# A fused graph layer on one core: results leave in block order, and the second half of the n gate is copied out of PSUM by ScalarE at once

## The chip, the cores and the metric

The kernel runs on one core of a Trainium2 chip. The metric is the device time of one execution in microseconds; for the kernel before it is the median of three runs. The engines are named as in the profile: PE is TensorE (PEld its weight loads), DVE is VectorE, ACT is ScalarE, POOL is GpSimd, and SP is SyncE, which here only issues DMAs.

## The reference, cut to what matters

For 64 graphs of 256 nodes with 256 channels each, one layer of a gated graph network is computed in float32:

```python
h   = maximum(layernorm(x), 0)                                  # x: (64, 256, 256)
c   = relu(bn1(conv1d_1tap(h)))
xc  = relu(bn2(conv1d_17taps(c)) + h)                           # along the 256 nodes
s   = h @ w_se.T + b_se                                         # 3 features per node
A   = exp(-|s_n - s_m|^2) * adj
xn  = A @ relu(h @ w_msg.T + b_msg)
gi  = concat(xc, xn) @ w_ih.T + b_ih                            # three gates of 256
gh  = h @ w_hh.T + b_hh
r   = sigmoid(gi_r + gh_r); z = sigmoid(gi_z + gh_z)
n   = tanh(gi_n + r * gh_n)
out = x + (1 - z) * n + z * h
```

## The kernel before, in words

**Tiling.** Graphs are worked on in pairs (a pair is called i, 32 of them), and four pairs make a block of eight graphs (b, 8 of them). A tile of a pair has channels on the 128 partitions, in two halves (dc 0 and 1), and 512 columns: the 256 nodes of one graph and then of the other. The nodes are not in their natural order there. The 17-tap convolution is done by a transform over 16 places in each half block of nodes, so that columns run in the order (q, h, b), while the rows of x and of the output in DRAM run in the order (b, h, c).

**The block.** The loop at line 1321 does the convolution of a block first: `begin(m)` and `complete(m)` (lines 941 and 948) multiply transformed inputs (tiles `Sv`, `V`, `U`, `PT`) with transformed filters. The filters were put in DRAM (`filt`) at the start by `filter_steps` and are loaded again for each block, one 128x512 tile after the other, into nine slots `wb` by `load_kinds` (line 905) on SP's queue. Then, pair by pair, come `sums`, the r and z gates and the n gate (`gates`, line 1181). Each gate pair is a matrix product in a seven-product form (`seven`, line 1155) in two PSUM tiles of two banks each, `acc0` and `acc1`: `opened(0, A)` and `opened(1, E)` evict them. During the gates the nine slots `wb` hold sums, tanh values (`tz`) and a temporary (`e`). At the end of a block `give` (lines 1475 and 1476) frees them, and `load_kinds()` starts the loads for the next block's first products, which go into `acc0` and `acc1` again.

**The n gate.** The function `n` (line 1190) evicts one PSUM tile in two steps: ACT writes half 1 plus its bias to `gn`; DVE multiplies that with r; then DVE's second instruction reads half 0 of the same PSUM tile and adds it. Only after this last read may PE open a new sum in the tile. After tanh and three DVE instructions the result stands in `tr`, and ACT copies it as two planes of 16 bits each to `back` (lines 1202 to 1204).

**Delivery.** `finish` (line 1245) turns `back` on SP's queue by a DMA transpose into `gn`; `deliver` (line 1260) has ACT merge the 16-bit planes back into rows of float32 in `back`, and then POOL's queue adds x to them in flight (a load with `accum_op`, line 1268) and stores them (line 1269), per graph one load and one store of 256 KB. Both address DRAM through `rows` (line 588), a pattern of 8 by 16 pieces of 2 KB; `blocks` (line 609) has the same pieces in sequence. For the last pair of a block the delivery comes in the middle of the next block.

**What sets the order.** No instruction is issued where it is written. The `Recorder` (line 250) notes all of them, gives each a cost and, for DMAs, a size (lines 341 to 369), computes from the order of TensorE's work when each is due, plays a list schedule with these costs (`plan`, line 388), and emits in that order. An engine then works strictly in the order it was given. So a changed cost or a changed pattern can move instructions everywhere. `filter_steps` (line 1278) is called with (1, 2, 3, 3) steps after the first four pairs at the start.

Of the kernel before, what the change touches and what calls it, by code (L numbers as in the profile page):

```python
# [14 lines left out]
U16 = mybir.dt.uint16  # L15
AF = mybir.ActivationFunctionType
ALU = mybir.AluOpType
# [232 lines left out]
class Recorder:  # L250
# [83 lines left out]
    def record(self, engine, op, args, kw):  # L334
        method = getattr(getattr(self.nc, engine), op)
        out = kw["out"] if "out" in kw else args[0]
        ins = [v for v in list(args) + list(kw.values()) if isinstance(v, bass.AP) and v is not out]
        n = 1
        for s in out.shape[1:]:
            n *= s  # L340
        size = 0
        if op.startswith("dma"):
            if "transpose" in op:
                size, cost = 2.5, self.TURN
            elif "accum_op" in kw:
                size, cost = 2.3, 1.0
            else:
                k = max(self.share(out, ins[0]), 10 if engine == "gpsimd" else 1)
                run = min(self.run(v) for v in (out, ins[0]))
                size = n * out.shape[0] * WIDTH[out.dtype] * 16 / k / 330e3 * max(1, 1400 / run)  # L350
                cost = 0.35 if k > 10 and run > 1024 else 0.62
        elif engine == "tensor":
            cost = n / 597 + 0.006
            if op == "transpose":
                cost = out.shape[-1] / 1170
            elif args[1].shape[0] < 32:
                cost = 0.23
        elif engine == "vector":
            cost = {"bn_stats": 0.33, "bn_aggr": 0.07}.get(op, n / 960 + 0.07)
            if op == "tensor_mul" and n == 256:  # L360
                cost = 0.5
        elif engine == "scalar":
            cost = n / 1400 + (0.2 if op == "activation" else 0.12)
            if out.dtype == U16:
                cost = n / 860
            elif len(out.shape) == 3 and op == "activation" and n == 256:
                cost = 0.49
        else:
            cost = 1.1 if self.planned == 0 else 7.0 if ALU.pow in args else 2.0
        k = len(self.tasks)  # L370
        self.tasks.append(Task(engine, lambda: method(*args, **kw), cost, size, self.first))  # L371
        self.last[engine] = k
        if self.behind is not None:
            self.tasks[k].preds.add(self.behind)
        if self.first is not None:
            self.first += 1
        for v in ins:
            self.access(k, v, False)
        self.access(k, out, True)
        return k  # L380
# [106 lines left out]
def kernel(  # L487
# [18 lines left out]
    nc = Recorder(tc.nc)  # L506
    P = 128
    B, N, D = x.shape
    G = 2
# [4 lines left out]
    DC = D // P  # L514
# [6 lines left out]
    L = 16  # L521
    NW = N // L
# [65 lines left out]
    def rows(t, g):  # L588
        return t[g].rearrange("(b h c) d -> h b (c d)", h=L // 2, c=MC)

    def row_tile(t, g):
        return t[:, g * MC:(g + 1) * MC, :].rearrange("p c d -> p (c d)")
# [5 lines left out]
    def chunk(t, g, c):  # L598
        return t[:, g * N + c * P:g * N + (c + 1) * P]
# [3 lines left out]
    X, ADJ, HT, XNM, STATS = {}, {}, {}, {}, {}  # L603
# [5 lines left out]
    def blocks(t, g):  # L609
        return t[g].rearrange("(b h c) d -> b h (c d)", h=L // 2, c=MC)  # L610
# [114 lines left out]
    p = aux()  # L725
# [449 lines left out]
    def halfs(p, k):  # L1175
        return p[:, :, k * N:(k + 1) * N]

    def pieces(t):
        return t.rearrange("p (g n) -> p g n", n=N)

    def gates(i, between=None):
        tr, gn = tr_tile, gn_tile
        tz = [slots[ROLE[f"tz{dc}"]].rearrange("p c d -> p (c d)") for dc in range(DC)]

        def rz(dc, p):
            for gate, t in ((0, tr[:, dc]), (1, tz[dc])):
                nc.scalar.activation(pieces(t), halfs(p, gate), AF.Tanh,
                                     bias=b_rz[:, gate * DC + dc:gate * DC + dc + 1], scale=0.5 - dc)

        def n(dc, p):  # L1190
            g = gn[:, dc]
            nc.scalar.activation(pieces(g), halfs(p, 1), AF.Identity,
                                 bias=b_hh[:, 2 * DC + dc:2 * DC + dc + 1], scale=1.0 - 2 * dc)
            nc.vector.scalar_tensor_tensor(g, tr[:, dc], 1.0, g, op0=ALU.add, op1=ALU.mult)
            nc.vector.scalar_tensor_tensor(pieces(g), pieces(g), 0.5, halfs(p, 0), op0=ALU.mult,
                                           op1=ALU.subtract if dc else ALU.add)
            nc.scalar.activation(g, g, AF.Tanh, bias=b_ih[:, 2 * DC + dc:2 * DC + dc + 1])
            d = tr[:, dc]
            nc.vector.tensor_sub(d, HT[i][:, dc], g)
            nc.vector.scalar_tensor_tensor(d, tz[dc], 1.0, d, op0=ALU.add, op1=ALU.mult)  # L1200
            nc.vector.scalar_tensor_tensor(d, d, 0.5, g, op0=ALU.mult, op1=ALU.add)
            u = d.bitcast(U16).rearrange("p (n j) -> p j n", j=2)
            for j in range(2):
                nc.scalar.copy(back.bitcast(U16).rearrange("p (c j n) -> p c j n", c=DC, j=2)[:, dc, j], u[:, j])

        def last(dc, g, p):
            a = slice(g * N, (g + 1) * N)
            v, d = gn[:, dc, a], tr[:, dc, a]
            nc.scalar.activation(v, p[:, N:], AF.Identity,
                                 bias=b_hh[:, 2 * DC + dc:2 * DC + dc + 1], scale=1.0 - 2 * dc)  # L1210
            nc.vector.scalar_tensor_tensor(v, d, 1.0, v, op0=ALU.add, op1=ALU.mult)
            nc.vector.scalar_tensor_tensor(v, v, 0.5, p[:, :N], op0=ALU.mult, op1=ALU.subtract if dc else ALU.add)
            nc.scalar.activation(v, v, AF.Tanh, bias=b_ih[:, 2 * DC + dc:2 * DC + dc + 1])
            nc.vector.tensor_sub(d, HT[i][:, dc, a], v)
            nc.vector.scalar_tensor_tensor(d, tz[dc][:, a], 1.0, d, op0=ALU.add, op1=ALU.mult)
            for c in range(MC):
                t = chunk(y_last[:, dc], g, c).rearrange("p (b h) -> p h b", b=NW)
                u, w = (q[:, c * P:(c + 1) * P].rearrange("p (h b) -> p h b", b=NW) for q in (d, v))
                nc.vector.scalar_tensor_tensor(t, u, 0.5, w, op0=ALU.mult, op1=ALU.add)

        seven(i, RZ, rz)
        if between:
            between()
        if i + 1 < NP:
            seven(i, NH, n)
            return
        a0, p5, e1, a1, e0 = aux(), aux(), aux(), acc()[:, 1], acc()[:, 0]
        e = slots[ROLE["e"]].rearrange("p c d -> p (c d)")
        part(a0, 1, i, NH, True)
        nc.scalar.mul(e0, a0, -1.0)  # L1230
        part(p5, 5, i, NH, True)
        nc.scalar.copy(e, p5)
        part(a0, 2, i, NH)
        last(0, 0, a0)
        part(e0, 6, i, NH)
        nc.vector.tensor_add(a1, e0, e)
        part(e0, 7, i, NH)
        nc.vector.scalar_tensor_tensor(e1, e0, -1.0, e, op0=ALU.mult, op1=ALU.subtract)
        last(1, 1, e1)
        part(a1, 3, i, NH)  # L1240
        last(0, 1, a1)
        part(e0, 4, i, NH)
        last(1, 0, e0)
# [16 lines left out]
    def deliver(i):  # L1260
        y = back.rearrange("p (q d) -> p q d", d=D)
        t = gn_tile.rearrange("p c n -> p (c n)").bitcast(U16)
        v = y.bitcast(U16).rearrange("p q (c d j) -> p j c q d", c=DC, j=2)
        u = t.rearrange("p (c j q d) -> p j c q d", j=2, c=DC, d=P)
        for j in range(2):
            nc.scalar.copy(v[:, j], u[:, j])
        for g in range(G):
            nc.gpsimd.dma_start(out=row_tile(y, g), in_=rows(x, G * i + g), accum_op=ALU.add)
            nc.gpsimd.dma_start(out=rows(out, G * i + g), in_=row_tile(y, g))

    FIRST = PARTS[1][1]
    steps = deque((m, g) for g in range(FIRST) for m in range(len(PASSES)))
# [5 lines left out]
    def filter_steps(n, wide=True):  # L1278
        for _ in range(n):
            banks[0] += 1  # L1280
            p = acc()[:, 0] if wide and banks[0] % 3 == 0 else aux()
            filters(p, *steps.popleft(), nc.gpsimd if len(steps) % 2 else nc.sync)
# [9 lines left out]
    for j in range(PB):  # L1292
        if j > 0:
            norm(j)
        transpose_h(j)
        conv1(j, True)
        split(j)
        filter_steps((1, 2, 3, 3)[j])
    *bn2, b_ih, b_hh = columns("bn2")
    s2, h2_shift = fold_bn(bn2, "bn2", 1.0 / L)  # L1300
    b_rz = keep("b_rz", 2 * DC)
# [19 lines left out]
    for b in range(NB):  # L1321
        i = b * PB
# [25 lines left out]
        if b == 0:  # L1348
# [6 lines left out]
            back = late.tile([P, DC * W], FP, name="back")  # L1355
# [168 lines left out]
```

## Time and profile before

| what | value |
|---|---|
| median of three runs | 1705.13 us |
| the three runs | 1708.3, 1705.13, 1702.14 us |
| the profiled execution: its own time | 1703.87 us |
| its span, first to last instruction | 1702.1 us |
| mean granted TensorE clock | 0.994 |
| DVE busy | 1457.8 us (86%) |
| ACT busy | 1052.4 us (62%) |
| POOL busy | 231.8 us (14%) |
| DMA moved | 261.47 MB, mean 154 GB/s |

The profile is of one execution. A row of a group names the tile that is written and the tiles that are read; then come the number of instructions, the microseconds that they were busy together, the mean nanoseconds of one, and the idle time of the engine just before them with what ended it. A row of a timeline has the start, the length, the engine, the instruction, how many were merged, and in brackets the idle time before it. Since one helper records everything, every instruction has the same line, L371; groups are told apart by their tiles.

### The profile page before, as it was taken

The numbers are of one execution on the slowest core, as the hardware profiler recorded it, in microseconds if no ns is written. First come the engines' busy times: TensorE is split into PE (matmuls) and PEld (weight loads), VectorE is DVE, ScalarE is ACT, GpSimd is POOL, SyncE is SP. The second block draws the span as 40 slices with busy tenths as digits, with TensorE's granted clock in tenths as the row PEclk, the third lists the DMA queues.
The fourth block names the chain that finished last, engine by engine and source line by source line (L and its number), as shares of the span: only waits on it lengthen the run. The fifth ranks groups of instructions, "written<-read, shape, count | busy, mean of one in ns | idle before, by whom it ended". The sixth has DMA issues, their size and how long they took to land.

```text
span 1702.1 us, 26181 instructions
## 1 busy us (share of the span) xinstructions
PE 1666.3 (98%) x8984; PEld 1420.8 (83%) x8984; DVE 1457.8 (86%) x3401; ACT 1052.4 (62%) x1967; POOL 231.8 (14%) x245
## 2 busy tenths in 40 slices
PE   8999999999999999999999999999999999999998
PEld 5888878988889788888888887897888978898886
DVE  7969989799889998799997998979987899879545
ACT  5546665685657765676655866567575766556453
POOL 4211130022110121102110021101211012100010
PEclk9999999999999999999999999999999999999999
DMA  9982666966579366773559554694756836484032
GB/s 228 306 280 69 137 117 142 280 136 140 108 196 241 94 127 124 218 208 89 122 113 293 136 116 110 160 273 97 144 112 191 233 91 125 88 245 129 17 60 52
DMA packets 326812, 261.47 MB, mean 154 GB/s; under 512 B 204751, under 2 KB 252139, under 8 KB 326678
## 3 DMA queue, kind: packets, MB, share of 16 engines
q1 hardware_dynamic: 296982, 216.71, 48.4%
q0 software_dynamic: 29280, 42.76, 13.1%
q8 instruction: 71, 1.16, 0.3%
q14 instruction: 63, 0.52, 0.1%
q10 hardware_dynamic: 416, 0.32, 0.1%
HBM read 156.60 MB, written 43.78 MB: 118 GB/s over the span
## 4 chain that ended last, share of the span: by engine, by line
PE 77%; DVE 17%; DMA 3%; issue 1%; ACT 1%; SPq 0%; DVEq 0%; ACTq 0%
PE acc L371 52%; PE aux L371 25%; DVE V L371 3%; DVE T L371 3%; DVE U L371 2%; DVE gn L371 2%; DMA wb<-filt 2%; DVE tr L371 1%; DVE acc L371 1%; DVE wb L371 1%; DVE Yv L371 1%; DVE PT L371 1%; DMA taps<-in_c_wT_dram 1%; DVE msg L371 1%; DMA filt<-Yv 0%
## 5 line engine op out<-in xcount | busy, mean ns | idle before, releaser
L371 PE MATMUL acc<-wb,w_ih 128*128 128x256 f32 x768 | 191.9, 379 | 0.0
L371 PEld LDWEIGHTS acc<-wb,w_ih 128*128 128x128 f32 x768 | 145.9, 190 | 19.8
L371 POOL DMA_DIRECT2D back<-in_x_dram x62 | 61.9, 1161 | 696.6 <-ACT back L371 622.5
L371 POOL TENSOR_TENSOR rstd<-rstd,neg_half 128x4 f32<-128x4 f32 x32 | 81.6, 2548 | 472.7 <-DVE shift L371 284.8
L371 PE MATMUL aux<-wb,w_x 128*128 128x256 f32 x576 | 141.6, 384 | 0.6 <-ACT e L371 0.5
L371 DVE SCALAR_TENSOR_TENSOR V<-T,V 128x128 f32<-128x128 f32 (+2 forms) x448 | 140.2, 377 | 0.0
L371 PE MATMUL acc<-wb,w_x 128*128 128x256 f32 x576 | 136.5, 381 | 1.8 <-DVE acc L371 1.5
L371 PEld LDWEIGHTS acc<-wb,w_x 128*128 128x128 f32 x576 | 107.9, 190 | 28.6 <-DVE acc L371 8.4
L371 PEld LDWEIGHTS aux<-wb,w_x 128*128 128x128 f32 x576 | 108.0, 191 | 20.2 <-issue 4.0
L371 PE MATMUL aux<-w_msg,hT 128*128 128x259 f32 x512 | 120.9, 381 | 0.0
L371 PE MATMUL acc<-V,wb 128*128 128x128 f32 x1024 | 119.0, 275 | 0.6 <-ACT acc L371 0.6
L371 PEld LDWEIGHTS acc<-U,wb 128*128 128x128 f32 x1024 | 117.4, 192 | 1.5 <-issue 0.5
L371 PE MATMUL acc<-U,wb 128*128 128x128 f32 x1024 | 118.2, 275 | 0.3 <-DMA wb<-filt 0.3
L371 PEld LDWEIGHTS acc<-V,wb 128*128 128x128 f32 x1024 | 116.7, 192 | 1.2 <-ACT acc L371 0.8
L371 PE MATMUL acc<-wb,w_hh 128*128 128x256 f32 x384 | 110.1, 381 | 0.7 <-ACT acc L371 0.7
L371 DVE TENSOR_TENSOR T<-Yv 128x512 f32<-128x512 f32 (+1 forms) x80 | 42.5, 580 | 79.4 <-ACT Yv L371 78.9
L371 PE MATMUL aux<-hT,w_c 128*128 128x512 f32 x224 | 107.3, 595 | 2.7 <-ACT e L371 2.7
L371 PE MATMUL acc<-Yv,w_ih 128*128 128x256 f32 x380 | 108.5, 381 | 0.1
L371 PEld LDWEIGHTS aux<-w_msg,hT 128*128 128x128 f32 x512 | 96.5, 190 | 14.3
L371 PE MATMUL acc<-hT,w_hh 128*128 128x256 f32 x380 | 104.7, 383 | 0.6 <-ACT acc L371 0.4
L371 PE MATMUL acc<-xnm,w_ih 128*128 128x256 f32 x380 | 103.9, 380 | 0.0
L371 ACT COPY back<-gn 128x1024 uint16<-128x1024 uint16 x62 | 80.5, 1348 | 36.6 <-DMA gn<-back 36.6
(194 smaller groups left out, 3842.1 us busy)
## 6 DMA issues: line engine op xcount, KB each, us to landing
wb<-filt SPq DMA_DIRECT2D x376, 256.0 KB
back<-in_x_dram POOLq DMA_DIRECT2D x62, 256.0 KB, 7.3
out_dram<-back POOLq DMA_DIRECT2D x62, 256.0 KB, 4.8
x<-in_x_dram SPq DMA_DIRECT2D x58, 256.0 KB
halves_d<-halves SPq DMA_DIRECT2D x28, 512.0 KB
adjh<-halves_d SPq DMA_DIRECT2D x112, 128.0 KB
hh<-halves SPq DMA_DIRECT2D x108, 128.0 KB
filt<-Yv POOLq DMA_DIRECT2D x18, 224.0 KB, 4.6
```

Of the source, the lines that this page charges most:

```text
L371: self.tasks.append(Task(engine, lambda: method(*args, **kw), cost, size, self.first))
```

## The change

Four things change. `deliver` addresses x and the output through `blocks`; for this the two copies of `n` into `back` permute the columns, from the order (q, h, b) that they read to (q, b, h), while they wrote and read them in sequence before. `n` gets a second ACT instruction that copies half 0 of the PSUM tile to the pair's `XNM` tile, whose products are over by then, and DVE's second instruction reads that copy. The planner is told a size of 1.3 in place of 2.3 for an accumulating load. And the calls of `filter_steps` at the start take (0, 2, 3, 4) steps.

```diff
             elif "accum_op" in kw:
-                size, cost = 2.3, 1.0
+                size, cost = 1.3, 1.0
...
             nc.scalar.activation(pieces(g), halfs(p, 1), AF.Identity,
                                  bias=b_hh[:, 2 * DC + dc:2 * DC + dc + 1], scale=1.0 - 2 * dc)
+            x = XNM[i][:, dc]
+            nc.scalar.copy(pieces(x), halfs(p, 0))
             nc.vector.scalar_tensor_tensor(g, tr[:, dc], 1.0, g, op0=ALU.add, op1=ALU.mult)
-            nc.vector.scalar_tensor_tensor(pieces(g), pieces(g), 0.5, halfs(p, 0), op0=ALU.mult,
-                                           op1=ALU.subtract if dc else ALU.add)
+            nc.vector.scalar_tensor_tensor(g, g, 0.5, x, op0=ALU.mult, op1=ALU.subtract if dc else ALU.add)
...
             u = d.bitcast(U16).rearrange("p (n j) -> p j n", j=2)
+            v = back.bitcast(U16).rearrange("p (c j n) -> p c j n", c=DC, j=2)[:, dc]
             for j in range(2):
-                nc.scalar.copy(back.bitcast(U16).rearrange("p (c j n) -> p c j n", c=DC, j=2)[:, dc, j], u[:, j])
+                nc.scalar.copy(v[:, j].rearrange("p (q b h) -> p q b h", h=L // 2, b=NW),
+                               u[:, j].rearrange("p (q h b) -> p q b h", h=L // 2, b=NW))
...
         for g in range(G):
-            nc.gpsimd.dma_start(out=row_tile(y, g), in_=rows(x, G * i + g), accum_op=ALU.add)
-            nc.gpsimd.dma_start(out=rows(out, G * i + g), in_=row_tile(y, g))
+            nc.gpsimd.dma_start(out=row_tile(y, g), in_=blocks(x, G * i + g), accum_op=ALU.add)
+            nc.gpsimd.dma_start(out=blocks(out, G * i + g), in_=row_tile(y, g))
...
         split(j)
-        filter_steps((1, 2, 3, 3)[j])
+        filter_steps((0, 2, 3, 4)[j])
```

## The prediction

> **What bounds the kernel now.** I read the page's busy times first, then PE's groups with their idle time, then timelines where PE stands still.
>
> ```profile
> PE 1666.3 (98%) x8984; PEld 1420.8 (83%) x8984; DVE 1457.8 (86%) x3401; ACT 1052.4 (62%) x1967; POOL 231.8 (14%) x245
> ```
>
> PE is busy for 98% of the span: 1702.1 less 1666.3 leaves 35.8 us of visible idle time, and PE's work is the same in both kernels. So nothing that only speeds DVE, ACT or a DMA can bring more than a part of these 35.8 us. Where they lie, PE's groups by form say:
>
> ```profile
> L371 PE MATMUL acc<-Sv,wb 128*128 128x128 f32 x512 | 67.2, 288 | 14.2 <-DVE tr L371 9.4 <-DMA wb<-filt 2.8 <-DVE gn L371 1.8
> ```
>
> 14.2 us stand before the products that open a block. In PE's timeline the seven block entries (b = 1 to 7) show gaps of 1.75, 2.28, 1.95, 2.40, 2.36, 2.36 and 0.24 us. Three things must be there: the tile acc0 must be free, the first filter must have landed, and PE must be done. The chain of work at the third entry shows which comes last:
>
> ```profile
> 691.05 0.88 PE acc L371 x4
> ...
> 691.94 5.68 DMA wb<-filt
> 697.62 0.14 issue
> 697.76 2.38 PE acc L371 x10
> ```
>
> The filter takes 5.68 us to land. DVE's last read of acc0 is over well before that, so the row's "DVE tr" names an instruction that ended at that moment by chance:
>
> ```profile
> 695.28 0.68 DVE L371 SCALAR_TENSOR_TENSOR gn<-gn,acc 128x512 f32<-128x512 f32 x1
> ```
>
> It ends at 695.96. Why the filter is slow, the queues tell, first for the third entry (POOL, then SP), then for the seventh (POOL, SP, PE):
>
> ```profile
> 684.78 1.96 POOL L371 DMA_DIRECT2D back<-in_x_dram  x2 [27.12 <-ACT back L371]
> 691.27 0.64 POOL L371 DMA_DIRECT2D out_dram<-back  x1 [4.52 <-DMA back<-in_x_dram]
> 693.00 0.63 POOL L371 DMA_DIRECT2D out_dram<-back  x1 [1.09 <-DMA back<-in_x_dram]
> ```
> ```profile
> 691.51 3.92 SPq L371 DMA_DIRECT2D wb<-filt  x7
> ```
> ```profile
> 1493.24 0.64 POOL L371 DMA_DIRECT2D out_dram<-back  x1 [4.54 <-DMA back<-in_x_dram]
> 1494.91 0.63 POOL L371 DMA_DIRECT2D out_dram<-back  x1 [1.03 <-DMA back<-in_x_dram]
> ```
> ```profile
> 1498.02 8.74 SPq L371 DMA_DIRECT2D wb<-filt  x11
> ```
> ```profile
> 1502.56 2.92 PE L371 MATMUL acc<-Sv,wb 128*128 128x128 f32 x24 [0.24 <-issue]
> 1506.05 1.16 PE L371 MATMUL acc<-Sv,wb 128*128 128x128 f32 x8 [0.58 <-DMA wb<-filt]
> ```
>
> At the third entry both stores of the pair before are issued just as the filters are: from the first filter issue (691.51) to the first product (697.76) it takes 6.25 us. At the seventh the stores are 3 to 5 us earlier, and it takes 4.54 us. The 1.7 us between is the gap.
>
> **What the Trainium skill says.** "DMA: Bandwidth & Descriptors", section "Why a DMA increments its semaphore by 16 and not by 1": a DMA runs on the largest number of engines up to 16 that divides the slowest dimension of both sides. The 8x16 pieces of `rows` then give 8 engines, the 128 of `blocks` 16. The trace doesn't name engines; its landing times agree in direction (the block-order load of adj on POOL's queue, also 256 KB, lands in 3.5 us at the median, a store in `rows` order in 4.8, an accumulating load in 7.3). Same page, "Issuing engines are not separate DMA queues": all queues share 16 engines, which fits the two entries above. "Advanced Engine Details and Errata", section "SBUF Cachelines": accesses that go to a new line of 16 bytes each time pay a penalty. The trace shows it on DVE alone (below). "ScalarE: Activation LUTs", section "What ACT_TABLE_LOAD costs": an activation without pointer operands takes 186 ns and 0.833 ns an element, 612 ns for 512; the copies into back take 618.
>
> **The change part by part.**
>
> *Block order, at the entries.* The seventh entry's own rest is 0.24 + 0.58 = 0.82 us. If the other six come to it, they give 13.1 - 6 x 0.82 = 8.2 us. Do the stores get out of the way? A load with accumulation at the third entry takes about 6.2 us from issue (684.78) to the store that waits for it (691.27), 7.6 with its pair (685.4 to 693.00). With twice the engines I put it between the 3.5 us of the adj load and 6.2, at 4.8; so the stores are issued some 1.4 to 2 us earlier, and they take less long themselves. In the new emission order ACT's first merging copy also stands ahead of `wb<-aux`, before which ACT idles 5.69 us. That is 2 to 4 us in all, against the 1.7 us needed. It can't be below nothing: no byte is added.
>
> *PSUM copied at once.* 62 more ACT copies; the row wb<-aux (PSUM, 512 columns) has 584 ns, and successive instructions overlap, so some 0.49 us each, 30 us of ACT in all. DVE's instruction costs the same from SBUF (gn<-tr,gn 681 ns) as from PSUM (677). acc0 comes free before PE's last product of the block instead of at 695.96; but the filter, not acc0, is last, and once the filter comes at 4.5 us (696.0) the two would tie. So this part gains nothing alone, and lets the first one gain in full. Behind the copy in ACT's queue waits the tanh of n; who waits for that is DVE's tail of the gate, not PE.
>
> *The permuted copies.* 124 copies read 16-bit elements 64 bytes apart instead of 4.
>
> ```profile
> L371 ACT COPY back<-tr x124: 596/618/632, 194.0 to 1671.4; 128x512 uint16<-128x512 uint16 x124
> ```
> ```profile
> L371 DVE TENSOR_TENSOR e<-e,adj 128x256 f32<-128x256 f32 x128 | 68.9, 593 | 5.6 <-ACT e L371 5.5
> L371 DVE TENSOR_TENSOR wb<-wb,hT 128x256 f32<-128x256 f32 x64 | 26.6, 416 | 0.1
> ```
>
> The first DVE row reads adj at steps of 64 bytes, the second reads in sequence: 177 ns more for 256 elements, 0.69 ns each. On 512 elements that is 0.35 us, a copy of 0.97. Against it, ACT reads PSUM at steps of 32 bytes without loss (adjh<-aux 592 ns, wb<-aux 584). Nothing shows ACT reading SBUF so; the bounds are 0.62 and, at three times the skill's rate per element (an estimate), 186 + 3 x 0.833 x 512 = 1.47 us. I take 0.8, the middle between no penalty and DVE's. Four of these stand together, and the worst place for them is ahead of the exponentials of `affinity`, for which PE already waits 0.45 us in seven places:
>
> ```profile
> 634.22 1.35 ACT L371 COPY hT<-hh 128x1024 uint16<-128x1024 uint16 x1 [0.15 <-DVE tr L371]
> 635.44 0.57 ACT L371 COPY wb<-aux 128x512 f32<-128x512 f32 x1
> 635.91 1.36 ACT L371 COPY hT<-hh 128x1024 uint16<-128x1024 uint16 x1
> 637.12 2.18 ACT L371 COPY back<-tr 128x512 uint16<-128x512 uint16 x4
> 640.44 1.21 ACT L371 ACTIVATE e<-aux 128x256 f32<-128x256 f32 x4 [1.15 <-PE aux L371]
> ```
>
> The cover is the 1.15 us of idle time. The PSUM copy takes 0.49 of it, less the 0.15 idle before hT: 0.81 us are left for four copies, so nothing is lost up to 0.62 + 0.20 = 0.82 us a copy. At 0.8 I count nothing here, and 1 us in all for smaller slips elsewhere.
>
> *The start and the planner.* PE works the same products at the start; the stall for taps before 18.82 us stays, since the first filter step still stands ahead of the second conv1. The smaller size moves a transpose of gn in SP's queue from among the filter loads to behind adjh; the copies that need it come some 5 us later than it lands. Nothing, give or take 2 us.
>
> **Sum.** -8.2 + 1 = -7.2 us. The profiled execution's own time is 1703.87 (span 1702.1 and 1.8 around it): 1696.7. It stands 1.3 below the median; from the median, 1705.1 - 7.2 = 1697.9, so 1698.
>
> **The rivals.**
>
> *The copies cost about 1.0 us each.* Each affinity then loses 4 x 0.37 - 0.81 = 0.7 us, 5 us in seven places, and the entries' gain is nearly used up: 1705.1 - 8.2 + 5 + 1 = 1703. For it: DVE's rows. Against: ACT's PSUM rows.
>
> *Slower: the copies cost up to 1.47 us, and ACT comes late with the exponentials.* Each affinity loses 4 x 0.85 - 0.81 = 2.6 us, 18 us in all; two copies ahead of ACT's negation of A add about 2 more over the blocks. 1705.1 - 8.2 + 20 = 1717. It decides from about 1.15 us a copy on, where 7 x (4 x 0.53 - 0.81) = 9 us passes the gain. ACT's slack against PE is small in every gate, which speaks for it.
>
> *The entries don't change.* If filter loads are slow for their own sake (seven are issued within 4 us) and not for the stores, only the small slips remain: 1706. Against it: the seventh entry.
>
> **How the numbers follow.** Forecast 0.43, copies at 1.0 us 0.25, slow copies 0.22, entries unchanged 0.10. I take 0.3% (5 us) as what a measurement of this kernel can tell from no change. Faster: four fifths of the first and a third of the second, 0.43. Slower: nearly all of the third, a tenth of the others, 0.29. Within: 0.28. The range: down to 1690 if the entries lose everything (14.2 us), up to 1716, near the slow case; about 0.2 lies outside. As both signs hold much, the likeliest case's own range is 1693 to 1702.
>
> **What would show it.** The row acc<-Sv has 4 to 7 us of idle time in place of 14.2; back<-in_x lands in about 5 us; back<-tr takes about 0.8 us; PE's wait for ACT's e stays at about 0.45 us a place. I am wrong if back<-tr is over 1.1 us with PE waiting 1 us or more for e, or if the entry gaps are still 2 us with the stores out of the way.

## The result, and the profile after

The changed kernel takes 1707.56 us (median of 12 runs, 1702.29 to 1710.2) against 1705.95 us of the kernel before (median of 12 runs): a ratio of 1.0007, 95% interval 0.9996 to 1.0017. No difference can be told. 1698 was forecast, and the chances leaned to faster. Both things that the forecast argued about did happen: the block entries became free, and ACT became late. The second ate the first.

The page of the changed kernel, first the engines' busy time, then the DMA issues of POOL with their median time from issue to landing; the last two lines are those of the kernel before:

```profile
PE 1666.4 (98%) x8984; PEld 1420.9 (83%) x8984; DVE 1459.8 (86%) x3401; ACT 1134.3 (67%) x2029; POOL 241.0 (14%) x245
...
back<-in_x_dram POOLq DMA_DIRECT2D x62, 256.0 KB, 5.1
out_dram<-back POOLq DMA_DIRECT2D x62, 256.0 KB, 2.6
```
```profile
back<-in_x_dram POOLq DMA_DIRECT2D x62, 256.0 KB, 7.3
out_dram<-back POOLq DMA_DIRECT2D x62, 256.0 KB, 4.8
```

PE does the same work in the same time. ACT is busy for 82 us more (1134.3 for 1052.4): by their rows the PSUM copies take 35.9 us, and the copies into `back` 126.5 in place of 68.9 (neighbours overlap in part, so the rows add up to more). The loads with accumulation land in 5.1 us for 7.3 before, the stores in 2.6 for 4.8. At the third block entry the two loads and the two stores of POOL, and SP's first filter loads, now stand so:

```profile
691.96 1.80 POOL L371 DMA_DIRECT2D back<-in_x_dram  x2 [29.61 <-ACT back L371]
696.26 0.58 POOL L371 DMA_DIRECT2D out_dram<-back  x1 [2.50 <-DMA back<-in_x_dram]
698.03 0.57 POOL L371 DMA_DIRECT2D out_dram<-back  x1 [1.19 <-DMA back<-in_x_dram]
```
```profile
700.08 3.86 SPq L371 DMA_DIRECT2D wb<-filt  x7
```
```profile
703.34 1.04 PE L371 MATMUL aux<-w_msg,hT 128*128 128x259 f32 x4
704.22 3.73 PE L371 MATMUL acc<-Sv,wb 128*128 128x128 f32 x32
```

The stores are issued 3.8 and 2.1 us ahead of the first filter load, where before they were issued with it, and the block's first product follows 4.14 us after that load (6.25 before) with no gap at all. So much for the gain. What PE waits for now, and then two of the same rows in the kernel before; each row has what PE was about to write, the engine and tile that it waited for, then the total in us, how many times, and the longest:

```profile
PE aux L371 <- ACT e L371: 10.0, 10, 1.5
...
PE acc L371 <- ACT acc L371: 3.4, 2, 2.7
PE acc L371 <- ACT Yv L371: 3.3, 4, 1.4
PE aux L371 <- ACT zT L371: 3.0, 3, 1.6
...
PE acc L371 <- DMA wb<-filt: 1.6, 4, 0.8
```
```profile
PE aux L371 <- ACT e L371: 3.2, 7, 0.5
...
PE acc L371 <- ACT acc L371: 1.7, 3, 0.7
```

In the kernel before, `Yv` has no row and `zT` 0.8 us. The waits for ACT grew from 5.7 to 20.2 us (0.5 us in a further row for `zT` included); the idle time before `acc<-Sv` fell from 14.2 to 5.4 us, of which 3.3 are the new waits for `Yv`:

```profile
L371 PE MATMUL acc<-Sv,wb 128*128 128x128 f32 x512 | 67.1, 286 | 5.4 <-ACT Yv L371 3.3 <-DMA wb<-filt 1.6 <-ACT zT L371 0.5
```

The cause is in the copies' row, and the place is the same as in the forecast, four copies ahead of the exponentials of `affinity` (first ACT's timeline, then PE's, and last PE's at the same place in the kernel before):

```profile
L371 ACT COPY back<-tr x124: 1042/1077/1112, 195.1 to 1674.5; 128x512 uint16<-128x512 uint16 x124
```
```profile
643.31 3.96 ACT L371 COPY back<-tr 128x512 uint16<-128x512 uint16 x4
647.17 1.21 ACT L371 ACTIVATE e<-aux 128x256 f32<-128x256 f32 x4
```
```profile
647.61 1.71 PE L371 MATMUL aux<-hT,w_c 128*128 128x512 f32 x2 [1.54 <-ACT e L371]
```
```profile
640.88 1.13 PE L371 MATMUL aux<-hT,w_c 128*128 128x512 f32 x2 [0.45 <-ACT e L371]
```

A copy takes 1.08 us, not 0.62 and not the 0.8 of the forecast. ACT has no idle time left ahead of the exponentials (1.15 us before), and PE waits 1.54 us for them where it waited 0.45. A second place is new. In the middle of a block's first products two copies of the second channel half (dc 1) stand ahead of ACT's evictions of `acc` into `Yv`, which PE needs to open the tile again:

```profile
511.39 2.02 ACT L371 COPY back<-tr 128x512 uint16<-128x512 uint16 x2
513.43 1.07 ACT L371 COPY Yv<-acc 128x512 f32<-128x512 f32 x2
```
```profile
514.56 3.50 PE L371 MATMUL acc<-Sv,wb 128*128 128x128 f32 x16 [1.36 <-ACT Yv L371]
```

In the kernel before all four copies stood together and earlier (501.49 to 503.67), and this wait did not exist:

```profile
501.49 2.18 ACT L371 COPY back<-tr 128x512 uint16<-128x512 uint16 x4
```

### The profile page after: what moved, and what is told of

Read it like the earlier page. It is cut to its first block, busy times and chain, and to the rows that moved or that the text cites. A ratio compares the mean times of both kernels' runs of the same rounds, so it can differ in the third digit from the quotient of the medians.

```text
span 1704.4 us, 26235 instructions
## 1 busy us (share of the span) xinstructions
PE 1666.4 (98%) x8984; PEld 1420.9 (83%) x8984; DVE 1459.8 (86%) x3401; ACT 1134.3 (67%) x2029; POOL 241.0 (14%) x245
## 4 chain that ended last, share of the span: by engine, by line
PE 80%; DVE 8%; ACT 6%; DMA 3%; issue 1%; SPq 0%; ACTq 0%; DVEq 0%
PE acc L371 54%; PE aux L371 26%; ACT back L371 2%; DMA wb<-filt 1%; DVE V L371 1%; DVE tr L371 1%; ACT zT L371 1%; ACT gn L371 1%; DVE T L371 1%; DVE gn L371 1%; DMA taps<-in_c_wT_dram 1%; DVE U L371 1%; DVE wb L371 1%; DVE st L371 1%; ACT Yv L371 1%
## 5 line engine op out<-in xcount | busy, mean ns | idle before, releaser
L371 POOL DMA_DIRECT2D back<-in_x_dram x62 | 56.7, 1059 | 773.7 <-ACT back L371 743.6
L371 POOL TENSOR_TENSOR rstd<-rstd,neg_half 128x4 f32<-128x4 f32 x32 | 92.7, 2896 | 437.1 <-DVE shift L371 240.7
L371 ACT COPY back<-tr 128x512 uint16<-128x512 uint16 x124 | 126.5, 1076 | 17.1 <-DVE tr L371 16.8
L371 PE MATMUL aux<-e,msg 128*128 128x256 f32 x448 | 103.3, 379 | 0.0
```

## The experiments

Four theories. **A**: the permuted copies' length is the price, paid where they stand ahead of something PE waits for. **B**: the 62 PSUM copies make ACT late. **C**: the new order that the planner writes costs the gain. **D**: it is the PSUM copy, not the block order, that freed the entries. Ratios below are to the kernel before, run beside each kernel; 0.0006 is 1 us, and differences in us are worked out from the ratios.

**The granted clock.** Each execution has its mean granted TensorE clock on record, and the time goes with it: of the changed kernel's 12 executions the two at 0.996 took 1702.29 and 1704.84 us, the one at 0.991 took 1710.2. Fitted within each version, over all executions but those of the write in steps below, 0.001 of the clock goes with 1.3 us (an estimate). Leaving that version out, both kernels and five of the versions ran at means of 0.9922 to 0.9930, six others at 0.9939 to 0.9949. Where this matters, the difference at an equal clock stands beside the measured one, as an estimate from these figures. A second check is PE's visible idle time, span less busy time, of the one profiled execution: 35.8 us before, 38.0 us after. Why six versions ran at a higher clock isn't shown; it may itself come from their edits.

### The copies' length, in the changed kernel's own order

First with the permutation left out:

```diff
-                nc.scalar.copy(v[:, j].rearrange("p (q b h) -> p q b h", h=L // 2, b=NW),
-                               u[:, j].rearrange("p (q h b) -> p q b h", h=L // 2, b=NW))
+                nc.scalar.copy(v[:, j], u[:, j])
```

> The changed kernel with the two copies into back reading in sequence again; every instruction stands in the same place, only the permutation is left out (nodes leave in the wrong places of the output). Theory A (the permuted copies, 1.08 us instead of 0.62 each, stand ahead of the exponentials and of the negation of A and so make PE wait): back<-tr falls to 0.62 us, PE's waits for ACT's e fall from 10.0 to about 3 us and its waits for ACT's Yv from 3.3 to under 1; together 8 to 10 us less, so about 1698. Theory B (the 62 PSUM copies make ACT late) and theory C (the new order of the planner costs the gain): the order and the PSUM copies are unchanged, so within 2 us of the changed kernel, 1706 to 1708.

Measured: 1694.51 us, ratio 0.9925 (0.991 to 0.9941). PE's waits:

```profile
PE aux L371 <- ACT e L371: 4.5, 10, 0.5
PE acc L371 <- DMA wb<-filt: 4.0, 7, 1.2
...
PE acc L371 <- ACT acc L371: 3.0, 3, 1.9
```

No wait for `Yv` is left, and those for `e` are back at 0.45 us a place. B and C fall as the main cause: PSUM copies and order are those of the changed kernel. Against the changed kernel it is 0.0082 less, with both intervals 14 us, give or take 3: more than the 8 to 10 expected. The clock has a part in it (a mean of 0.9942 for 0.9930): at an equal clock it is some 11 us, and PE's visible idle time fell by 6.6 us, from 38.0 to 31.4.

Then the same permutation with the loop the other way, reading in sequence and writing in steps of 16 bytes:

```diff
-... v[:, j].rearrange("p (q b h) -> p q b h", ...), u[:, j].rearrange("p (q h b) -> p q b h", ...)
+... v[:, j].rearrange("p (q b h) -> p q h b", ...), u[:, j].rearrange("p (q h b) -> p q h b", ...)
```

> The changed kernel, same permutation and same output, but the loop of the two copies runs the other way: they read in sequence and write elements 16 bytes apart. Theory A: what counts is the copy's length. If writing in steps costs no more than the merging copies' rate (1345 ns for 1024 elements written 4 bytes apart: some 0.77 us for 512), PE's waits for e come down to about 4 us and the time to about 1699; if stepped writes cost as much as stepped reads (1.08 us), nothing changes, 1707. Theories B and C: no change whatever the copies take, 1706 to 1708.

Measured: 1888.53 us (median of all six executions), ratio 1.105 (1.1011 to 1.1089). Neither length that I had foreseen came; the row of the copies, and PE's waits:

```profile
L371 ACT COPY back<-tr x124: 2455/2750/2822, 194.7 to 1860.7; 128x512 uint16<-128x512 uint16 x124
```
```profile
PE acc L371 <- ACT wb L371: 39.0, 11, 5.3
PE aux L371 <- ACT e L371: 36.2, 10, 6.8
PE acc L371 <- ACT Yv L371: 35.2, 11, 5.2
```

A write in steps costs far more than a read in steps (2.75 us against 1.08). That the time follows the copies' length, in the same places and with nothing else moved, is A's point; three lengths of 0.62, 1.08 and 2.75 us give 1694.5, 1707.6 and 1888.5 us. The last step isn't all waiting: the profiled execution is 187 us longer than the changed kernel's, of which PE's visible idle time is 128 (165.7 for 38.0) and its busy time 59 (1725.5 for 1666.4), at a granted clock of 0.953 for 0.994.

### The other parts, taken out of the changed kernel

Without the PSUM copy (the planner's order moves a little with it):

```diff
-            x = XNM[i][:, dc]
-            nc.scalar.copy(pieces(x), halfs(p, 0))
...
-            nc.vector.scalar_tensor_tensor(g, g, 0.5, x, op0=ALU.mult, op1=ALU.subtract if dc else ALU.add)
+            nc.vector.scalar_tensor_tensor(pieces(g), pieces(g), 0.5, halfs(p, 0), op0=ALU.mult,
+                                           op1=ALU.subtract if dc else ALU.add)
```

> The changed kernel without the ACT copy of half 0 out of PSUM: DVE reads PSUM as before. Theory A: ACT is relieved of 0.5 us ahead of some exponentials and the entries stall again by at most 0.5 us each on the late read of acc0: the two about cancel, 1703 to 1709. Theory B: the 36 us of PSUM copies are what makes ACT late, so PE's waits for ACT fall from 21 to under 13 us and the time to 1697 to 1700. Theory D (the entries were freed by the PSUM copy, not by the block order): idle time before acc<-Sv goes back to 12 us or more, 1712 or above.

Measured: 1705.3 us, ratio 0.9989 (0.9979 to 1.0). From its rows of waits:

```profile
PE aux L371 <- ACT e L371: 7.0, 10, 1.0
...
PE acc L371 <- issue: 1.7, 7, 0.2
```

The seven entries cost 0.24 us each (the row "issue"), so D falls. The waits for ACT fell to 12.9 us as B said, but the time not to B's 1697 to 1700: it is some 3 us (0.0018, give or take 2.6 us) under the changed kernel. Even that goes with the clock, 0.9945 for 0.9930: at an equal clock nothing is left of it, while PE's visible idle time is 36.0 us for 38.0. The longest wait for `e` is 1.0 us in place of 1.54: the PSUM copy's half microsecond.

With the planner's numbers of before (size 2.3, steps (1, 2, 3, 3)):

> The changed kernel with the planner's numbers of before: size 2.3 for an accumulating load and filter steps (1, 2, 3, 3). Theory A: only the start moves (it costs the changed kernel 0.6 to 0.95 us), so 1705 to 1708. Theory C: the order chosen with the new numbers costs several microseconds, among them the wait of 2.7 us at 217 and the one of 1.6 at 299, so 1700 to 1703.

Measured: 1707.86 us, ratio 1.0008 (0.9996 to 1.0021), the changed kernel's own. These numbers cost nothing that shows beside the rest, give or take 3 us.

### Each part alone, added to the kernel before

The block order alone (the planner is made to take the stores for what they were, so that no instruction moves):

```diff
-            nc.gpsimd.dma_start(out=row_tile(y, g), in_=rows(x, G * i + g), accum_op=ALU.add)
-            nc.gpsimd.dma_start(out=rows(out, G * i + g), in_=row_tile(y, g))
+            nc.gpsimd.dma_start(out=row_tile(y, g), in_=blocks(x, G * i + g), accum_op=ALU.add)
+            nc.gpsimd.dma_start(out=blocks(out, G * i + g), in_=row_tile(y, g))
```

> The kernel before with one thing changed: the accumulating loads and the stores address DRAM in block order. Every instruction of every engine keeps its place; the copies into back read in sequence, so the permutation is left out (nodes leave in the wrong places of the output). Theory A (stores and loads on more engines free the filter loads at the block entries, nothing else is needed): idle time before acc<-Sv falls from 14.2 to 3 to 6 us, time 8 to 11 us below before, 1695 to 1698. Theory D (acc0 must come free by the PSUM copy as well): the entries keep 1.5 us or more each on DVE's last read of acc0, 1702 to 1705.

Measured: 1694.72 us, ratio 0.9937 (0.9912 to 0.9962), 11 us less, as A expected. Its profiled execution took 1703.32 us, at a clock of 0.992, so only its waits are read here. The products that open a block, and those on `V` that follow:

```profile
L371 PE MATMUL acc<-Sv,wb 128*128 128x128 f32 x512 | 68.4, 288 | 3.1 <-issue 1.5 <-DMA wb<-filt 1.2 <-DVE gn L371 0.2
```
```profile
L371 PE MATMUL acc<-V,wb 128*128 128x128 f32 x1024 | 120.5, 276 | 5.1 <-DMA wb<-filt 4.1 <-ACT acc L371 0.8
```

14.2 us became 3.1 without any PSUM copy: D falls a second time. Not all of it is won: ahead of the products on `V` 5.1 us stand idle for 0.6 before, most of it for later filter loads, so PE's visible idle time fell by 7.4 us, from 35.8 to 28.4. That fits the measured 11 us once the clock is counted (0.9947 for 0.9922): at an equal clock some 8 us are left.

The permuted copies alone, again with every instruction in its old place:

> The kernel before with one thing changed: the two copies into back permute (1.08 us for 0.62). Every instruction keeps its place; DRAM is still addressed in the order of before, so nodes leave in the wrong places of the output. Theory A (the copies are the price, whatever the order): PE's waits for e grow from 0.45 to about 1.5 us in seven places and some come at the negation of A; 8 to 13 us more than before, 1714 to 1719. Theory C (the price belongs to the changed kernel's order, in which the copies stand badly): at most 3 us more than before, up to 1709.

Measured: 1712.43 us, ratio 1.0032 (1.0019 to 1.0045), so 5.5 us more (3 to 8). Rows of PE's waits:

```profile
PE acc L371 <- DVE tr L371: 9.4, 4, 2.4
PE aux L371 <- ACT e L371: 6.5, 7, 1.0
...
PE acc L371 <- ACT acc L371: 3.4, 3, 2.1
```

Between the two theories. The copies cost time in the old order too, but less than half of the 14 us (half of the 11 at an equal clock): six waits for `e` grew by 0.55 us each and not by 1.09, and none came for `Yv`. The wait for ACT's `acc` near 220 us grew from 0.41 to 2.14 us, as it did in the changed kernel. Here is C's share: the price of one and the same copy depends on what stands beside it. By PE's visible idle time the share is smaller, 5.1 us here (40.9 for 35.8) against 6.6 there.

The PSUM copy alone (62 more instructions on ACT, with which the planner moves others, so this is not the order of before):

> The kernel before with the ACT copy out of PSUM alone. Theory A: ACT loses 0.5 us ahead of each exponential's copies where 1.15 us are idle, so PE loses nothing there; the entries wait for the filter as before, 12 us or more; 1705 to 1708. Theory B (36 us of ACT time reach PE): 1711 or above. Theory D (this copy frees the entries): idle time before acc<-Sv falls under 8 us, 1699 to 1701.

Measured: 1710.15 us, ratio 1.0022 (1.0011 to 1.0033): 3.8 us more. The entries' row:

```profile
L371 PE MATMUL acc<-Sv,wb 128*128 128x128 f32 x512 | 72.4, 297 | 12.9 <-DMA wb<-filt 10.8 <-ACT z L371 1.7 <-ACT xnm L371 0.4
```

This row also answers a question of the forecast: with acc0 free early, the profile names the filter load at the entries and no longer "DVE tr". The entries did wait for the filters. But the copy is neither free, as A had it, nor quite as dear as B had it. PE's waits for DVE's `acc` grew from 1.5 to 3.6 us in the order that it brings, but others shrank, and PE's visible idle time is 36.6 us, only 0.8 more; the rest of its price isn't located.

### Told the true cost, and two versions

The changed kernel, its planner told 1.08 us for a permuted copy:

```diff
             if out.dtype == U16:
-                cost = n / 860
+                cost = n / (475 if len(out.shape) == 4 else 860)
```

> The changed kernel with the planner told what a permuted copy takes (1.08 us in place of 0.60): same instructions, new order. Theory A: what hurts is that the plan puts copies that it takes for short ahead of exponentials and negations; told the truth, it puts them where ACT idles, PE's waits for ACT fall from 20 to 12 us or less, 1698 to 1703. Theory C (any new plan from these tables slips elsewhere): PE's waits only change places, 1705 to 1712.

Measured: 1703.62 us, ratio 0.998 (0.997 to 0.9991): 3.4 us less than before, 4.6 less than the changed kernel. It measures faster than both, if little; but it ran at a mean clock of 0.9949, and at an equal clock it is level with the kernel before and some 1 us under the changed one, though PE's visible idle time fell to 29.9 us. At the same place as above ACT now has this order:

```profile
641.85 3.02 ACT L371 COPY back<-tr 128x512 uint16<-128x512 uint16 x3
644.77 0.66 ACT L371 ACTIVATE e<-aux 128x256 f32<-128x256 f32 x2
645.31 1.09 ACT L371 COPY back<-tr 128x512 uint16<-128x512 uint16 x1
646.26 0.68 ACT L371 ACTIVATE e<-aux 128x256 f32<-128x256 f32 x2
```

No wait for ACT's `e` is left in PE's rows; instead those for DVE's `acc` grew from 2.4 to 5.4 us. Both sides were half right. The true cost together with no PSUM copy was not measured.

The last four runs share a base of their own, in which plain copies take the place of the DMA transposes; each is read against that base.

> A new base for three kernels: the kernel before with its 86 DMA transposes replaced by plain DMA copies of the same bytes between the same tiles (so the transposition of results, adjacency and h is left out, and the output's values mean nothing); one ACT copy reads 16-bit elements 4 bytes apart that were in sequence. Every instruction keeps its place. If the transposes' own time isn't on the path (their results were there some 5 us early), within 5 us of before, 1701 to 1711. If plain copies of 2 KB rows take much longer or collide with filter loads, several microseconds more.

Measured: 1704.91 us, ratio 0.9991 (0.9982 to 1.0001): as good as the kernel before.

> The changed kernel with the same replacement of the DMA transposes by plain copies (transposition left out), every instruction in its place. All theories: it stands to g0_before as the changed kernel stands to before, 0 to 4 us above it, with PE waiting about 10 us for ACT's e and 3 for Yv.

Measured: 1706.45 us, ratio 0.9999 (0.9985 to 1.0013), 1.4 us above the base; PE waits 10.0 us for `e` and 2.3 for `Yv`. The base stands for the real pair.

> The kernel before with block order in DRAM and the permuted copies and nothing else, every instruction in the place that it has in the kernel before; DMA transposes replaced by plain copies as in g0_before. If the two add up (block order alone measured 11 us less than before, permuted copies alone 5.5 more), 4 to 7 us under g0_before. Theory A (the copies cost the 14 us that they cost in the changed kernel, once the entries no longer hide them): 1 to 4 us above g0_before. Theory C (the copies' price depends on where the plan puts them): 4 to 7 us under g0_before, PE's waits for e about 1.0 us in seven places and none for Yv.

Measured: 1698.27 us, ratio 0.9954 (0.9938 to 0.997): 6.3 us under the base, give or take 3. The first row of its waits:

```profile
PE aux L371 <- ACT e L371: 6.5, 7, 1.0
```

The two parts add up (-11 and +5.5; at an equal clock -8 and +5.5, for -3 here, whose clock was 0.9946 for the base's 0.9924), and 1.0 us in six places for `e` with none for `Yv` is what C said. Of the versions that permute the results this is the best, and it lacks the PSUM copy. With its DMA transposes it was not measured.

> A version of the changed kernel in which the permutation is made where ACT reads PSUM: the evictions of r, z and both halves of n read PSUM in the new order (steps of 64 bytes), h is read in steps by DVE's subtraction, and the copies into back read in sequence. Nothing else moves; DMA transposes are replaced by plain copies as in g0_before. Theory A (only the copies' length costs the time): evictions stay at 0.58 to 0.69 us, as adjh<-aux did in steps of 32 bytes, back<-tr falls to 0.62, DVE's 62 subtractions grow by 0.35 us each, of which PE sees 2 to 5 us; so 4 to 10 us under g0_before. Against it: if stepped reads of PSUM take ACT as long as stepped reads of SBUF (0.46 us more each, 248 evictions), 13 us or more above g0_before.

Its core, with the halves of a PSUM tile laid out in turns of 128 columns so that one instruction can read them:

```diff
+            return (t.rearrange("p (q b h) -> p q b h", h=L // 2, b=NW),
+                    p.rearrange("p q (h b) -> p q b h", h=L // 2))
...
-            nc.scalar.copy(pieces(x), halfs(p, 0))
+            nc.scalar.copy(*turned(x, halfs(p, 0)))
...
-            nc.vector.tensor_sub(d, HT[i][:, dc], g)
+            nc.vector.tensor_sub(q[0], HT[i][:, dc].rearrange("p (q h b) -> p q b h", h=L // 2, b=NW), q[1])
```

Measured: 1703.58 us, ratio 0.9987 (0.9974 to 1.0): 0.7 us under the base, 2 under its changed kernel, so less than expected (its clock was 0.9939; at an equal clock it is about 1 us over the base). ACT's evictions and PE's first rows of waits; then DVE's subtraction:

```profile
L371 ACT ACTIVATE gn<-acc,bn_columns 128x512 f32<-128x512 f32 x62 | 42.6, 687 | 81.3 <-PE acc L371 77.6 <-DVE acc L371 2.7
L371 ACT COPY xnm<-acc 128x512 f32<-128x512 f32 x62 | 35.8, 577 | 0.0
```
```profile
PE acc L371 <- DVE acc L371: 10.1, 20, 1.3
PE aux L371 <- ACT e L371: 4.5, 10, 0.5
```
```profile
L371 DVE TENSOR_TENSOR tr<-hT,gn 128x512 f32<-128x512 f32 x62 | 63.5, 1026 | 0.6 <-ACT gn L371 0.6
```

ACT reads PSUM in the new order for nothing (577 ns, as in the changed kernel), and `e` is back at 0.45 us. But DVE's subtraction takes 0.34 us longer, nearly the 0.35 expected, and DVE has no room for it there: PE's waits for DVE's `acc` are 10.1 us in 20 places, for 3.9 in 7 with the copies permuted. Theory A was too narrow in saying that only the copies' length counts; the engine that takes the permutation over pays for it.

## Why the prediction was wrong, point by point

**What bounds the kernel: right.** PE's work did not change, and its idle time was most of the stake; the granted clock, which the sum left out, goes with up to 3 us more.

**Block order at the entries: right in mechanism, and in size as far as the runs tell.** The forecast said -8.2 us, with 0.82 us left at an entry. Alone it brought 11 us (6 to 15), some 8 at an equal clock. The working hits this in part by luck: six entries cost 0.24 us, not 0.82, since the seventh, taken for the best that there can be, had a filter wait of its own; but 4.5 us more now stand idle ahead of the products on `V`, which the sum had left out. Loads landed in 4.1 us for the first and 5.5 for the second of a pair, against the 4.8 taken. (The 6.2 us "to the store that waits for it" is the time to the load's landing; the store starts 6.5 us after the issue.)

**The PSUM copy: wrong.** "Gains nothing alone" holds, but it costs: 3.8 us alone, in the order that it brings, and between nothing and about 3 in the changed kernel. The forecast charged its 0.49 us rightly at the exponentials, but as cover (idle time of ACT that may be used up before PE waits longer) that was free. Nor was it needed to "let the first one gain in full": the block order alone freed the entries.

**The permuted copies: the step that failed.** "I take 0.8, the middle between no penalty and DVE's." They take 1.08, and what was counted as nothing became the largest loss: 14 us in the changed kernel (some 11 at an equal clock), 5.5 alone. The reading behind it was that ACT, which reads PSUM in steps for nothing, might read SBUF almost so. It doesn't; DVE's rows, which also read SBUF, were the nearer ones and would have given 0.97. With 1.08 the forecast's own sum has 7 x (4 x 0.46 - 0.81) = 7.2 us for the exponentials, and comes to 1705. The rest of that step holds: the cover was put at 0.81 us for four copies, and PE's wait rose by 1.09 us where the copies rose by 4 x 0.46 = 1.84, so the cover was 0.75. Without the PSUM copy, in the old order, the wait rose by 0.55, a cover of 1.29: the 0.54 between fits the PSUM copy. The number of places is the other term: five at 1.54 us (and five at 0.45), not seven.

**Smaller slips, 1 us in all: wrong.** The second place was seen in the slow rival alone ("two copies ahead of ACT's negation of A"). In fact it is the eviction into `Yv` that they delay: 3.3 us in four places. And one wait of 2.7 us for ACT's `acc`, near 220 us, is 2.2 us shorter with short copies.

**Start and planner numbers: right,** nothing that shows, though only beside the other parts. **The rivals:** the one with copies of about 1.0 us was the case that came; its 1703 was 4.6 us too low; copies of 1.08 and not 0.99 us are 2.5 of it, and it lacked the second place and a price for the PSUM copy. Of the signs that the forecast named, two came as said (`acc<-Sv` idle for 5.4 us, loads in 5.1) and two did not (`back<-tr` at 1.08 us, `e` at 1.54). Its line for being wrong, copies over 1.1 us, lay just too high.

What stays open: why the changed kernel's order makes the copies dearer than the old one is shown in its parts (the exponentials and `Yv`; the one wait near 220 us comes in both), but not how much of the new order comes from the PSUM copy and how much from the stores being planned as shorter. That the PSUM copy with its new order costs 3.8 us alone is measured; where, is not. Nor is it shown why some versions were granted a higher clock.

## What to carry to other kernels

Before a permutation is given to an engine that has idle time on average, measure or price the stepped access on that engine and memory, and multiply by how many of the instructions stand together ahead of something the bounding engine waits for. Two changes that each fit into the same idle microsecond don't both fit: add up what stands in front of one wait. And a gain in one stage should be tried alone; here the block order with fewer companions gave more than the whole change. Where differences are a few microseconds in 1700, compare the granted clocks before a wait is made the cause.

## What the runs showed of the hardware

- ACT reading 16-bit elements of SBUF 64 bytes apart: 1077 ns for 512, against 618 when 4 bytes apart, 0.90 ns more each. Writing them 16 bytes apart (and reading 4 bytes apart): 2750 ns, 4.2 ns more each. The Trainium skill, "Advanced Engine Details and Errata", section "SBUF Cachelines", has a penalty for each access to a new line; both agree in direction, and the write's is over four times the read's.
- ACT reading 4-byte elements of PSUM 64 bytes apart: 577 and 687 ns for 512 columns, the same as in sequence.
- DVE reading one operand from SBUF 64 bytes apart: 1026 ns for 512 against 681, 0.67 ns more each.
- A 256 KB store in block order lands in 2.6 us for 4.8, the accumulating load in 5.1 for 7.3, with no byte less (2.5 and 5.0 where the block order is the only change).
- Within one version, 0.001 of the mean granted clock goes with 1.3 us of 1700 (an estimate from all executions). With the copies at 2750 ns and PE's visible idle time at 165.7 us, the granted clock of the profiled execution was 0.953, and the same matrix products took 1725.5 us for 1666.4.
